# Attention over heads in a four-layer transformer: projections copied into another ring, later marks for statistics and gates, and the last two tiles of tokens woven together

## The chip, the cores and the metric

The kernel runs on one core of a Trainium2 chip. The metric is the time of one execution on the device in microseconds (us). Three runs of the kernel before gave 2483.38, 2484.43 and 2485.16 us; their median is 2484.43 us. The profile comes from a further execution.

## The reference

The input x has 4 batches of 512 tokens with 288 channels; four layers follow one another. Every layer makes six vectors from a condition, normalises, attends, multiplies by a gate and adds, then does the same with an MLP of 1152 hidden channels (layer 0 has four experts, of which each token takes two). Layers 0, 1 and 3 attend over tokens. Layer 2 attends over heads: for each token the 16 heads of 18 channels attend to one another, and the result is transposed and reshaped across tokens. Cut to what matters:

```python
def layer_2(x, c):
    ada = silu(c) @ ada_w + ada_b
    shift_msa, scale_msa, gate_msa, shift_mlp, scale_mlp, gate_mlp = split(ada, 6)
    x = x + gate_msa * attention(modulate(layernorm(x), shift_msa, scale_msa))
    x = x + gate_mlp * mlp(modulate(layernorm(x), shift_mlp, scale_mlp))
    return x

def attention(x):
    qkv = (x @ qkv_w + qkv_b).reshape(n, t, 3, 16, 18)
    q, k, v = qkv[:, :, 0], qkv[:, :, 1], qkv[:, :, 2]
    attn = softmax(einsum('nthd,ntkd->nthk', q * 18 ** -0.5, k))
    out = einsum('nthk,ntkd->nthd', attn, v)
    out = out.transpose(0, 2, 1, 3).reshape(n, t, d)
    return out @ proj_w + proj_b
```

## The kernel before, in words

All values are float32, and x stays on chip. A batch is four tiles of 128 tokens, so there are 16 tiles. Instructions are issued in an order which the program itself sets: loops over the large work (attention of a layer, half MLPs of two tiles) call `gap()` (L139) at every block, and `gap` and `follow` (L152) put pieces of other work into these places. That other work consists of generators: a list of tasks with due times, and for layer 2 the lists `chain` and `beside`. A generator yields the cost that it has used up; `follow` adds a credit at each gap (RATE, 1.1 us, L52) and takes pieces while credit is left. `mark(key, delay)` (L99) says that a value is ready so many gaps later, and `until` (L920) holds a generator back until then. So a mark shifts where in each engine's program an instruction stands; every engine runs its own program in order.

Attention over heads is `attention_over_heads` (L809). It runs beside the MLP of layer 1 (batches 1 to 3) and that of layer 2, both written by `half_mlp` (L1638): nine hidden blocks, for each an `up` (L1650, and L1657 for the last channels; ACT's gelu L1661) and a `down` (L1669, L1672), and at the end the copy upd_m by ACT (L1683), its gating (L1684) and its addition to x (L1685) on GpSimd.

For each tile i, with heads in four groups g:

- `kept` (L822, matmuls L829): three groups of matmuls on TensorE give queries, keys and values; keys and values are copied by ACT (L838), queries are read where they are.
- `weigh`: VectorE multiplies queries and keys (pq, L847) and reduces the products to scores (hs, L853). The scores have a ring of three buffers (L845, tag "hs").
- `shift`: VectorE finds the maximum (L857) and subtracts it (L858). After every second tile ACT takes the exponentials of both (L1001).
- `weighted`: GpSimd multiplies weights and values (pv, L863; ring "ex" of four buffers). `summed`: VectorE reduces them (ho, L875). `denominators`: VectorE (L879, L880). `finish`: GpSimd divides (ho, L887) and SP writes the tile to a scratch area in DRAM (L888).

`stream` (L961) orders this: in its round i it weighs tile i, multiplies values for tile i − 2 and sums tile i − 3. After the last tile of a batch, `after(b)` (L940) reads the rows back from the scratch area (`read`, L892), transposes them (`turned`, L905), projects them (`project`, L912) with a copy upd_a by ACT (L916), gates (L917) and adds to x (L918), and then starts the norm for the layer's MLP. `before(b)` does the norm ahead of the attention. `norm` (L429) takes statistics on VectorE (L435, L436), their scalars on GpSimd (L443 to L446) and the scaling on ACT (L458); `chunks` (L486) transposes its result on TensorE (L501).

The copies upd_a and upd_m share the ring "upd" of two buffers. Layer 3's attention, which begins while layer 2 ends, writes queries and keys through a ring "qc" of three buffers, from which SP spreads them by transfers (L598). Its weights are loaded by `load_attention` (L228, transfers L247 to L256), and its first scores and maxima are L608 and L623. `gating` (L399, matmuls L406, copies L407) makes the gates and `modulation` (L367; L351, L357, L359, L389, L391) the six vectors.

The rounds of the stream that the diff replaces end with

```python
                if i >= 3:
                    finish(i - 3)
                    if (i - 3) % TB == TB - 1:
                        beside.append([after((i - 3) // TB), False])
```

Of the kernel before, what the change touches and what calls it, by code (L numbers as in the profile page):

```python
# [10 lines left out]
F32 = mybir.dt.float32  # L11
# [8 lines left out]
P = 128  # L20
# [38 lines left out]
def tile_dit_blocks(ctx: ExitStack, tc: tile.TileContext, x_in, cond_t, sel_den, sel_b, w_gate, layers, out):  # L59
# [39 lines left out]
    def mark(key, delay=1):  # L99
        ready[key] = flow["now"] + delay  # L100
# [708 lines left out]
    def attention_over_heads(l):  # L809
# [50 lines left out]
        def weighted(i, g):  # L860
            hs = slice(g * GH, (g + 1) * GH)
            prod = work.tile([P, GH, HD, NH], F32, tag="ex", bufs=4, name=f"pv_{l}_{i}_{g}")
            nc.gpsimd.tensor_tensor(  # L863
                prod,
                sc[i][:, hs, :].unsqueeze(2).to_broadcast([P, GH, HD, NH]),
                qkv[i][:, 1].rearrange("p h d -> p d h").unsqueeze(1).to_broadcast([P, GH, HD, NH]),
                ALU.mult,
            )
            pv[i, g] = prod

        def summed(i, g):
            hs = slice(g * GH, (g + 1) * GH)
            if g == 0:
                o[i] = work.tile([P, NH, HD], F32, tag="ho", bufs=2, name=f"ho_{l}_{i}")
            nc.vector.tensor_reduce(o[i][:, hs, :], pv.pop((i, g)), AX.X, ALU.add)  # L875

        def denominators(i):
            den = o["den", i] = small.tile([P, NH, 1], F32, tag="hd1", name=f"hd1_{l}_{i}")
            nc.vector.tensor_reduce(den, sc[i], AX.X, ALU.add)  # L879
            nc.vector.reciprocal(den, den)  # L880
# [27 lines left out]
        def project(b, t):  # L908
            pp = other()[:, :C]
            for k in range(NK):  # L910
                n = KP + (1 if k == NK - 1 else 0)
                nc.tensor.matmul(  # L912
                    pp, rt[b][:n, k, t * P : (t + 1) * P], w["wp"][:n, k, :], start=k == 0, stop=k == NK - 1
                )
            upd = work.tile([P, 2, C], F32, tag="upd", bufs=2, name=f"upd_a_{l}_{b}_{t}")
            nc.scalar.copy(upd[:, 0, :], pp)  # L916
            nc.gpsimd.tensor_tensor(upd[:, 0, :], upd[:, 0, :], gates[l, 0][:, b, :], ALU.mult)  # L917
            nc.gpsimd.tensor_tensor(x[:, b * TB + t, :], x[:, b * TB + t, :], upd[:, 0, :], ALU.add)  # L918

        def until(*keys):  # L920
            while any(ready.get(key, 1 << 30) > flow["now"] for key in keys):
# [18 lines left out]
        def after(b):  # L940

            for _ in range(3):
                yield WAIT
            read(b)
            for _ in range(3):
                yield WAIT
            yield from until(("gate", l, 0), ("projection", l))
            for k in range(NK):
                yield BANK
                turned(b, k)  # L950
                yield -0.9
            for t in range(TB):
                yield BANK
                project(b, t)
                yield -1.5
            mark(("x", l, 1, b), 6)
            yield from until(("x", l, 1, b))
            yield from norm(l, 1, b)
            yield from turn_normed(1, b)

        def stream():  # L961
            n = len(tiles)
            yield from until(("loaded", l), ("ht", l, 0, 0))
            for s in (1, 2, 0):
                if s:
                    yield BANK
                kept(0, s)
                yield -1.5
            beside.append([before(1), False])
            yield from until(("values free", l - 1, B - 1, TB - 1))  # L970
            del ready["cleared"]
            for i in range(n + 3):
                for g in range(4):
                    if i < n:
                        weigh(i, g)
                        yield 2.8
                        if g > 0 and i + 1 < n:
                            yield from until(("ht", l, 0, (i + 1) // TB))
                            if g < 3:
                                yield BANK  # L980
                            kept(i + 1, g % 3)
                            yield -1.5
                    if g == 1 and 2 <= i < n + 2:
                        denominators(i - 2)
                        yield 0.7
                    if i >= 3:
                        summed(i - 3, g)
                    if 2 <= i < n + 2:
                        weighted(i - 2, g)
                    yield 1.4 if i >= 3 else 0.0  # L990
                if i >= 3:
                    finish(i - 3)
                    if (i - 3) % TB == TB - 1:
                        beside.append([after((i - 3) // TB), False])
                if i < n:
                    shift(i)
                    if i % TB == TB - 2:
                        mark(("first products", l, i // TB), 1)
                    if i % 2:
                        for j in (i - 1, i):  # L1000
                            nc.scalar.activation(sc[j], sc[j], AF.Exp)  # L1001
                    yield 1.0
                if i % TB == 0 and 2 <= i // TB + 1 < B:
                    beside.append([before(i // TB + 1), False])
            mark(("over heads", l))
            mark(("all spread", l))
            yield from clear()
# [630 lines left out]
    def half_mlp(l, b, half, hook=None):  # L1638

        h, w, gate = ht[l, 1, b], w_mlp[l, 0], gates[l, 1]  # L1640
        func = AF.Gelu if l == 2 else AF.Gelu_apprx_tanh
        PY, UP = 0, 2
        US = 0.3
        s = slice(half * BT, (half + 1) * BT)

        def up(fs):
            for j, f in enumerate(fs):
                full = w["w1"][f // 3][0]
                for k in range(KF):
                    nc.tensor.matmul(  # L1650
                        banks[:, UP + j, :BT], full[:, k, (f % 3) * P : (f % 3 + 1) * P], h[:, k, s],
                        start=k == 0, stop=False,
                    )
                gap(US)
            for j, f in enumerate(fs):
                r = slice((f % 3) * RC, (f % 3 + 1) * RC)
                nc.tensor.matmul(banks[:, UP + j, :BT], w["w1"][f // 3][1][r, :], h[r, KF, s], start=False, stop=True)  # L1657
            hid = []
            for j, f in enumerate(fs):
                t = work.tile([P, S], F32, tag="ot", bufs=7, name=f"hid_{l}_{b}_{half}_{f}")[:, :BT]  # L1660
                nc.scalar.activation(t, banks[:, UP + j, :BT], func, bias=w["b1"][:, f : f + 1])  # L1661
                hid.append(t)
            return hid

        def down(fs, hid):
            if fs[0] == 0:
                for t in range(2):
                    r = slice(t * HP, t * HP + 1)
                    nc.tensor.matmul(banks[:, PY + t, :C], ones[r, :], w["b2"][r, :], start=True, stop=False)  # L1669
            for f, hf in zip(fs, hid):  # L1670
                for t in range(2):
                    nc.tensor.matmul(  # L1672
                        banks[:, PY + t, :C], hf[:, t * P : (t + 1) * P], w["w2"][f // 3][:, f % 3, :],
                        start=False, stop=f == NF - 1,
                    )
                if f < NF - 1:
                    gap(US)
                if hook is not None and f % 3 == 2:
                    hook(f // 3)
            if fs[-1] == NF - 1:  # L1680
                t0 = b * TB + 2 * half
                y = work.tile([P, 2, C], F32, tag="upd", bufs=2, name=f"upd_m_{l}_{b}_{half}")
                nc.scalar.copy(y, banks[:, PY : PY + 2, :C])  # L1683
                nc.gpsimd.tensor_tensor(y, y, gate[:, b : b + 1, :].to_broadcast([P, 2, C]), ALU.mult)  # L1684
                nc.gpsimd.tensor_tensor(x[:, t0 : t0 + 2, :], x[:, t0 : t0 + 2, :], y, ALU.add)  # L1685
                if half == 1:
                    mark(("x", l + 1, 0, b), 5)
                gap(US)

        for fs in DUOS:  # L1690
            hid = up(fs)
            if pending_down:
                pending_down.pop()()
            pending_down.append(lambda fs=fs, hid=hid: down(fs, hid))
# [28 lines left out]
    for l in range(n_layers):  # L1723
# [15 lines left out]
        if l == 1:  # L1739
            before.append(("token mod", B - 1))  # L1740
        task(products, base + 40, [("ada", l, 1, 3)] + before, modulation(l, 1))
        before = [("x", l, 0, B - 1)] if l else []
        task(products, base + 60, [("gate row", l, 1)] + before, gating(l, 1))
        if l == OVER_HEADS:
            due = starts["attention", l - 1] + 2 * (LEAD + N_STEPS - 14)
# [181 lines left out]
```

## Time and profile before

| | |
|---|---|
| median of three runs | 2484.43 us (2483.38 to 2485.16) |
| the profiled execution | 2486.91 us, of which its span is 2485.2 us |
| TensorE busy (PE) | 2291.2 us, 92% of the span |
| weights loaded to TensorE (PEld) | 1218.6 us, 49% |
| VectorE busy (DVE) | 1086.3 us, 44% |
| ScalarE busy (ACT) | 834.8 us, 34% |
| GpSimd busy (POOL) | 521.4 us, 21% |
| first multiplication of tile 0, of tile 15 of layer 2's attention | at 1369.83 us, at 1714.36 us |
| last finish of a tile (L887) | ends at 1780.35 us |
| first scores of layer 3 (L608) | at 1945.54 us |

Times are microseconds from the start of the span. A line of a timeline has the start, the duration, the engine, the line in the code, the operation, what it writes and reads with the shapes, and in brackets how long the engine was idle before it and who released it. SPq is SP's queue of transfers. A line of waits has the engine and line that waited, for whom, the sum in us, how often and the longest. The page's second part cuts the span in 40 slices; a digit is a slice's busy share in tenths.

### The profile page before, as it was taken

The numbers are of one execution on the slowest core, as the hardware profiler recorded it, in microseconds if no ns is written. First come the engines' busy times: TensorE is split into PE (matmuls) and PEld (weight loads), VectorE is DVE, ScalarE is ACT, GpSimd is POOL, SyncE is SP. The second block draws the span as 40 slices with busy tenths as digits, with TensorE's granted clock in tenths as the row PEclk, the third lists the DMA queues.
The fourth block names the chain that finished last, engine by engine and source line by source line (L and its number), as shares of the span: only waits on it lengthen the run. The fifth ranks groups of instructions, "written<-read, shape, count | busy, mean of one in ns | idle before, by whom it ended". The sixth has DMA issues, their size and how long they took to land. (4 is left out here: it accounts for less than half of the span.)

```text
span 2485.2 us, 30140 instructions
## 1 busy us (share of the span) xinstructions
PE 2291.2 (92%) x11188; PEld 1218.6 (49%) x11188; DVE 1086.3 (44%) x1955; ACT 834.8 (34%) x1233; POOL 521.4 (21%) x517
## 2 busy tenths in 40 slices
PE   5899999899998999999999999778589999999998
PEld 2333333367776773333353677455456433333455
DVE  2445655441012025555524669989210455555100
ACT  1244434422221223344426233323223244444311
POOL 2000020321022111100010257778621100011000
PEclk9699999999999997899999899888799799999999
DMA  5201110446554541000000001100110000000000
GB/s 143 97 30 62 38 36 12 107 161 189 177 160 152 175 124 62 13 14 16 28 21 1 22 3 32 36 17 17 22 56 2 28 16 16 14 14 6 1 20 20
DMA packets 163033, 134.23 MB, mean 54 GB/s; under 512 B 81365, under 2 KB 146725, under 8 KB 162886
## 3 DMA queue, kind: packets, MB, share of 16 engines
q1 hardware_dynamic: 159814, 122.86, 17.0%
q0 software_dynamic: 3072, 9.44, 1.2%
q8 instruction: 89, 1.46, 0.2%
q14 instruction: 58, 0.48, 0.1%
HBM read 90.67 MB, written 26.25 MB: 47 GB/s over the span
## 5 line engine op out<-in xcount | busy, mean ns | idle before, releaser
L660 DVE TENSOR_REDUCE mx<-banks 128x1 f32<-128x512 f32 x696 | 447.8, 685 | 370.9 <-PE banks L608 370.3
L608 PE MATMUL banks<-qk 32*128 32x512 f32 x3072 | 548.8, 681 | 11.8 <-DVE mx L660 7.0
L653 ACT ACTIVATE ex<-banks 128x1024 f32<-128x1024 f32 x348 | 356.4, 1024 | 513.2 <-PE banks L608 511.9
L608 PEld LDWEIGHTS banks<-qk 32*128 32x128 f32 x3072 | 180.5, 194 | 230.6 <-DVE mx L660 97.7
L863 POOL TENSOR_TENSOR pv<-hs,qk 128x1152 f32<-128x1152 f32 x64 | 203.7, 3196 | 50.2 <-DVE ho L875 35.3
L682 PE MATMUL banks<-ex,va 128*32 128x512 f32 x1536 | 212.2, 623 | 0.0
L1462 PE MATMUL banks<-w_b,hid_b 128*128 128x288 f32 x684 | 187.6, 417 | 0.0
L555 PE MATMUL banks<-ht,wqk 96*128 96x512 f32 (+1 forms) x360 | 186.7, 629 | 0.6 <-DVE upd_a L515 0.6
L1650 PE MATMUL banks<-ht,w 128*128 128x256 f32 x504 | 134.3, 402 | 38.2 <-ACT hid L1661 37.6
L1442 PE MATMUL banks<-block,w_b 128*128 128x256 f32 x684 | 165.8, 387 | 3.6 <-DMA w_b<-in_w 2.9
L702 POOL COPY rec<-r 128x512 f32<-128x512 f32 x48 | 29.6, 616 | 659.9 <-DVE r L698 586.2
L1672 PE MATMUL banks<-w,hid 128*128 128x288 f32 x504 | 151.8, 437 | 0.0
L1454 ACT ACTIVATE hid_b<-banks,b_b 128x256 f32<-128x256 f32 x171 | 68.7, 473 | 241.1 <-PE banks L1448 163.1
L1462 PEld LDWEIGHTS banks<-w_b,hid_b 128*128 128x128 f32 x684 | 123.9, 191 | 49.9 <-issue 21.9
L1442 PEld LDWEIGHTS banks<-block,w_b 128*128 128x128 f32 x684 | 129.3, 193 | 31.2 <-issue 11.4
L1650 PEld LDWEIGHTS banks<-ht,w 128*128 128x128 f32 x504 | 98.8, 201 | 61.7 <-ACT hid L1661 41.9
L719 PE MATMUL banks<-wp,ot 128*128 128x288 f32 x384 | 118.9, 435 | 5.9 <-DVE upd_a L515 3.5
L1672 PEld LDWEIGHTS banks<-w,hid 128*128 128x128 f32 x504 | 93.4, 198 | 46.3 <-issue 26.3
L516 POOL TENSOR_TENSOR x<-x,upd_a 128x288 f32<-128x288 f32 x48 | 38.1, 793 | 364.6 <-DVE upd_a L515 337.1
L555 PEld LDWEIGHTS banks<-ht,wqk 96*128 96x128 f32 (+1 forms) x360 | 61.4, 189 | 100.1 <-issue 86.2
L719 PEld LDWEIGHTS banks<-wp,ot 128*128 128x128 f32 x384 | 68.6, 195 | 76.1 <-issue 51.9
L682 PEld LDWEIGHTS banks<-ex,va 128*32 128x32 f32 x1536 | 31.1, 109 | 152.4 <-issue 150.6
(224 smaller groups left out, 2574.9 us busy)
## 6 DMA issues: line engine op xcount, KB each, us to landing
w_b<-in_w SPq DMA_DIRECT2D x57, 432.0 KB
w_b<-in_w SPq DMA_DIRECT2D x57, 384.0 KB
qk<-qc SPq DMA_DIRECT2D x336, 38.0 KB
wa<-in_wada SPq DMA_DIRECT2D x7, 864.0 KB
block<-x_mem SPq DMA_DIRECT2D x19, 288.0 KB
y_mem<-y_b SPq DMA_DIRECT2D x19, 288.0 KB
x_mem<-zeros SPq DMA_DIRECT2D x7, 768.0 KB
y_mem<-zeros SPq DMA_DIRECT2D x7, 768.0 KB
```

The source lines that it names most:

```text
L555: nc.tensor.matmul(to, st(rows, k), mv(rows, k), start=k == 0, stop=k == NK - 1)
L608: nc.tensor.matmul(to, qk[u][r, of, c * P : (c + 1) * P], qk[u][r, 1 - of, :], start=True, stop=True)
L653: nc.scalar.activation(e, WEIGHTS, AF.Exp)
L660: nc.vector.tensor_reduce(mxs[mu % 2][:, mc, h : h + 1], pm[j], AX.X, ALU.max)
L682: nc.tensor.matmul(SUMS[j * HP : (j + 1) * HP, :], vas[0][:, c, at : at + HP], ex[step, j // 2][:, j % 2, :], start=c == 0, stop=c == TB - 1,)
L719: nc.tensor.matmul(pp, done[b * NG + g][:, t * P : (t + 1) * P], w["wp"][:, g, :], start=g == 0, stop=g == NG - 1)
L863: nc.gpsimd.tensor_tensor(prod, sc[i][:, hs, :].unsqueeze(2).to_broadcast([P, GH, HD, NH]), qkv[i][:, 1].rearrange("p h d -> p d h").unsqu ...
L1442: nc.tensor.matmul(banks[:, UP + j, :BT], w1[:, k, j * P : (j + 1) * P], hx[i][:, k, :], start=k == 0, stop=False)
L1454: nc.scalar.activation(t, banks[:, UP + j, :BT], AF.Gelu_apprx_tanh, bias=b1[:, f : f + 1])
L1462: nc.tensor.matmul(banks[:, PY + t, :C], hid[j][:, t * P : (t + 1) * P], w2[:, j, :], start=f == 0, stop=f == NF - 1)
L1650: nc.tensor.matmul(banks[:, UP + j, :BT], full[:, k, (f % 3) * P : (f % 3 + 1) * P], h[:, k, s], start=k == 0, stop=False,)
L1672: nc.tensor.matmul(banks[:, PY + t, :C], hf[:, t * P : (t + 1) * P], w["w2"][f // 3][:, f % 3, :], start=False, stop=f == NF - 1,)
```

## The change

There are three parts. The projection's copy upd_a moves from the ring "upd" to the ring "qc". Marks come later: a batch's x after attention over heads from 6 to 9 gaps, x after the second half of a batch's MLP from 5 to 12 gaps, and a new mark "gated" 25 gaps after it, on which the second gates of layer 2 wait in place of x. The stream has one round less; in the ordinary rounds a group of sums comes ahead of the products with the values (`usual`), and the sums, products and finishes of the last tiles follow a table (`last`).

```diff
@@ project
-            upd = work.tile([P, 2, C], F32, tag="upd", bufs=2, name=f"upd_a_{l}_{b}_{t}")
-            nc.scalar.copy(upd[:, 0, :], pp)
-            nc.gpsimd.tensor_tensor(upd[:, 0, :], upd[:, 0, :], gates[l, 0][:, b, :], ALU.mult)
-            nc.gpsimd.tensor_tensor(x[:, b * TB + t, :], x[:, b * TB + t, :], upd[:, 0, :], ALU.add)
+            upd = work.tile([P, S], F32, tag="qc", bufs=3, name=f"upd_a_{l}_{b}_{t}")[:, :C]
+            nc.scalar.copy(upd, pp)
+            nc.gpsimd.tensor_tensor(upd, upd, gates[l, 0][:, b, :], ALU.mult)
+            nc.gpsimd.tensor_tensor(x[:, b * TB + t, :], x[:, b * TB + t, :], upd, ALU.add)
@@ after
-            mark(("x", l, 1, b), 6)
+            mark(("x", l, 1, b), 9)
@@ stream
-            for i in range(n + 3):
+            usual = {g: [f"s1{g}", f"w0{g}"] + (["d0"] if g == 1 else ["f1"] if g == 3 else []) for g in range(4)}
+            last = {
+                0: ["s30", "s31", "w00", "w01", "d0"], 1: ["s32", "s33", "f3", "w02", "w03", "s00", "w10"],
+                2: ["s01", "w11", "s02", "w12"], 3: ["d1", "s03", "w13", "f0"], 4: ["s10", "s11", "s12", "s13", "f1"],
+            }
+            for i in range(n + 2):
                 for g in range(4):
                     if i < n:
                         weigh(i, g)
...
-                    if g == 1 and 2 <= i < n + 2:
-                        denominators(i - 2)
-                        yield 0.7
-                    if i >= 3:
-                        summed(i - 3, g)
-                    if 2 <= i < n + 2:
-                        weighted(i - 2, g)
-                    yield 1.4 if i >= 3 else 0.0
-                if i >= 3:
-                    finish(i - 3)
-                    if (i - 3) % TB == TB - 1:
-                        beside.append([after((i - 3) // TB), False])
+                    for what in usual[g] if i < n else last.get((i - n) * 4 + g, ()):
+                        if i < n:
+                            j = i - 2 - int(what[1])
+                        else:
+                            j = n - 3 if what[1] == "3" or what == "f3" else n - 2 + int(what[1])
+                        if j < 0:
+                            continue
+                        if what[0] == "w":
+                            weighted(j, int(what[2]))
+                        elif what[0] == "s":
+                            summed(j, int(what[2]))
+                            yield 1.4
+                        elif what[0] == "d":
+                            denominators(j)
+                            yield 0.7
+                        else:
+                            finish(j)
+                            if j % TB == TB - 1:
+                                beside.append([after(j // TB), False])
@@ half_mlp
                 if half == 1:
-                    mark(("x", l + 1, 0, b), 5)
+                    mark(("x", l + 1, 0, b), 12)
+                    mark(("gated", l, b), 25)
@@ the tasks of each layer
-        before = [("x", l, 0, B - 1)] if l else []
+        before = [("gated", 1, B - 1) if l == OVER_HEADS else ("x", l, 0, B - 1)] if l else []
         task(products, base + 60, [("gate row", l, 1)] + before, gating(l, 1))
```

## The prediction, on record before the result

> **What bounds the kernel now.** I read the page first (parts 1 and 2), then a table of busy time by stretches, then the sums of waits, then the timelines of single engines around the longest waits.
>
> ```profile
> span 2485.2 us, 30140 instructions
> PE   5899999899998999999999999778589999999998
> DVE  2445655441012025555524669989210455555100
> POOL 2000020321022111100010257778621100011000
> ```
>
> A slice is 62 us. TensorE is at 9 tenths nearly everywhere, except in slices 26 to 30 (about 1550 to 1865 us). There VectorE and GpSimd stand at 7 to 9 tenths: this is the attention over heads of layer 2, beside the MLPs of layers 1 and 2. The stretches (columns: us, then busy time of PE, PEld, DVE, ACT, POOL with counts, clock, DMA share, GB/s) show where each limit rules:
>
> ```profile
> 1440.00:1460.00 20.00, 20.00 (x91) 14.40 (x91) 1.88 (x7) 4.47 (x10) 3.39 (x5) 1.00 0.00 1
> 1500.00:1580.00 80.00, 75.47 (x336) 52.75 (x336) 74.59 (x79) 26.93 (x51) 61.47 (x33) 0.97 0.26 49
> 1580.00:1620.00 40.00, 24.88 (x77) 17.34 (x77) 37.55 (x45) 12.86 (x24) 31.74 (x27) 0.76 0.07 8
> 1740.00:1780.00 40.00, 27.28 (x108) 19.51 (x107) 16.18 (x21) 10.59 (x20) 36.08 (x26) 0.84 0.07 8
> 1780.00:1800.00 20.00, 9.43 (x35) 6.29 (x34) 0.00 (x0) 3.17 (x5) 5.24 (x8) 0.67 0.43 50
> 1810.00:1945.00 135.00, 133.92 (x548) 90.89 (x544) 8.98 (x28) 40.49 (x82) 23.11 (x31) 0.96 0.11 34
> ```
>
> Up to 1580 TensorE is full but VectorE's chain of 16 tiles already sets the later end; from 1580 to 1740 VectorE is the limit (37.6 of 40), from 1740 to 1780 GpSimd (36.1 of 40), then SP's transfers, and from 1810 to 1945 TensorE again (133.9 of 135). So a microsecond on the stream of tiles before 1780 moves the end; TensorE work moved from before 1808 to after it does too.
>
> What VectorE waited for between 1360 and 1960 (us in total, times, longest):
>
> ```profile
> DVE st L435 <- POOL x L1685: 67.6, 4, 24.2
> DVE pq L847 <- PE banks L829: 18.8, 7, 5.0
> DVE hd L879 <- POOL ho L887: 10.6, 1, 10.6
> DVE hs L853 <- POOL pv L863: 8.8, 5, 2.4
> ```
>
> Of the 67.6 us only the first lies inside the stream (it ends at 1458.0, 18.5 us long); the others end at 1838.5, 1884.7 and 1907.1, when VectorE has nothing urgent. The places that matter (start, us, engine, line, and in brackets the idle time before with its releaser):
>
> ```profile
> 1458.02 0.46 DVE L435 BATCH_NORM_STATS2 st<-x 128x6 f32<-128x288 f32 x1 [18.52 <-POOL x L1685]
> 1476.73 1.36 DVE L847 TENSOR_TENSOR pq<-banks,qk 128x1152 f32<-128x1152 f32 x1 [4.31 <-PE banks L829]
> ...
> 1482.77 1.40 POOL L1684 TENSOR_TENSOR upd_m<-upd_m,gate 128x576 f32<-128x576 f32 x1 [9.81 <-ACT upd_m L1683]
> 1779.67 0.68 POOL L887 TENSOR_TENSOR ho<-ho,hd 128x288 f32<-128x288 f32 x1
> ...
> 1804.10 0.40 SPq L892 DMA_DIRECT2D rows<-scratch  x1
> 1808.29 1.06 PE L905 MATMUL banks<-ident,rows 128*96 128x128 f32 x4 [18.86 <-DMA rows<-scratch]
> ```
>
> The last line is the chain's hinge: the last tile's finish (L887) ends at 1780.35, SP then issues the weights of layer 3 (L247 to L256) until 1804.1, only then the read of the rows, and TensorE stands still 18.9 us for it.
>
> **What the Trainium skill says.** "Perfetto Trace Analysis", Optimization Strategy: a kernel can have regimes with different limiting engines, and gaps are to be sought on the limiting one within its regime; the table above agrees. "SBUF — State Buffer", SBUF: two separate sides: GpSimd and VectorE share one port pair as an exclusive lock, which a VectorE operation with two SBUF inputs needs. The trace agrees: the subtraction L858 takes 0.43 us alone and up to 3.2 us (3.18 at 1469.2) where pv (L863, 3.2 us) runs beside it. "TensorE: Matmul & The Clock Gate", What's actually happening: after idling the array runs at half clock for some microseconds; here the clock is 0.67 and lower between 1780 and 1810.
>
> **The change part by part.** I compared the instruction order of both kernels, engine by engine. Up to about 1436 us they are the same.
>
> *Later marks.* VectorE's order around the statistics of layer 2, batch 1, is unchanged: the 18.5 us stall at 1458 stays. What moves is on TensorE: the transposes of that batch go from after hidden block 3 to after block 7 of the running half MLP. In between lie: up 1.8, w1r 0.6, four blocks of down 4.1, up 1.0, w1r 0.6 (start to start in TensorE's timeline) = 8.1 us. The queries and keys of tile 4 (L829) follow: their third group ended at 1476.5, and now about 1485.4 (from block 8, due at 1476.8, with three groups of 1.5, up 1.9, w1r and bias 1.3, one block 1.1). Also, on GpSimd the update of x by the MLP (upd_m, 1.4 + 1.4 us) now stands ahead of pv of tile 1 (three of 3.2) and waits, as before, for ACT's copy, which comes about 1477.6. So pv of tile 1 ends at 1477.7 + 2.9 + 3 × 3.2 = 1490.2. VectorE's first reduction of tile 4 needs that buffer of scores (L845, three of them): 1490.3 against 1478.2, **+12.1 us**. (By TensorE alone it would be 8.9.) Queued behind it on VectorE is the whole stream.
>
> Of this, the later waits for L829 at tiles 5, 6 and 7 (1.5, 2.4 and 0.2 us in VectorE's timeline) vanish, since TensorE is then ahead: 12.1 − 4.2 = 7.9. The modulation's VectorE work moves from tile 8 to tile 10 (−2.65, then +2.1 and a wait of about 0.95): +0.4. The statistics of layer 3, batch 0, leave the tiles before the last exponentials (2.3 + 0.4 us): −2.7. The stream stands at **+5.6** when the last exponentials (before: 1738.4) run.
>
> *Gates later, first tiles.* A mark only shifts where instructions are issued; it adds no wait on the chip. VectorE's and TensorE's work is the same and in the sum above; on SP only the read of batch 0's rows moves, ahead of one write of tile 4, and nobody waits for that write. Their cover is TensorE's idle time (15 of 40 us at 1580 to 1620); without it some 5 us.
>
> *The burst.* GpSimd's work from the exponentials on is: 8 × 3.14 pv, 4 × 1.6 upd_a (L917, L918), two ho 1.3, statistics' scalars 1.9, the last ho 0.7 = 35.4, with small gaps 35.8. Before it took 41.9 (1738.4 to 1780.35), because the MLP's update, another norm and the wait for ACT stood ahead of the last ho: **−6.1**. GpSimd is full in both, so pulling VectorE's reductions forward saves nothing by itself. SP keeps its order, the weights ahead of the rows, so rows are read 23.8 us after the finish as before. Rows arrive at −0.5.
>
> *TensorE behind the rows.* Since TensorE's program puts the rows' transposes earlier in the layer-2 MLP (after block 0 of batch 1's second half, not after block 3), three blocks (3.2), two ups (3.6), w1r (0.6) and nine transposes (1.3) that ran in the shadow of the stall now come after it: **+8.7**. From there TensorE is full until 1945, so it counts whole. If that cover were gone already, nothing would be lost.
>
> *Copies in the ring of qc.* Where upd_a waited for its buffer before (L916, L1683: 3.7 and 3.4 us, at 1751 and 1760), TensorE had slack: no gain on the path. In the new ring the copies of batch 3 meet layer 3's q and k, whose tiles are free only when SP has sent them: 36 transfers in 38.2 us (L598). The third copy would come some 45 us after the rows, the fifth tile's transfers end near 50. ACT waits 5 us there and behind it is gelu, which TensorE needs; it has about two blocks in hand. Bounds 0 and 6, taken **+3**.
>
> *Layer 3's start.* 2.3 us of statistics and the gate copies go behind 24 maxima (L623), where VectorE is late: **−2** (bounds 0 and −3).
>
> Sum: 5.6 − 6.1 + 8.7 + 3 − 2 = **+9.2**. The profiled execution took 2486.91 us (span 2485.2 and 1.7 around it), 2.5 above the median of 2484.43. So 2496.1 in its own terms, and 2493.6, say 2493.5, beside the median. Differences under 0.2% (5 us) a measurement hardly tells from no change.
>
> **The rivals.**
> 1. *The stream makes its delay good and more* (faster). After tile 4 it still had waits: 9.5 for L829 (1.5, 2.4, 0.2, and 4.1 and 1.2 at tiles 13 and 15) and 8.8 for pv. If all go: 12.1 − 18.3 + 0.4 − 2.7 = −8.5, and with a free ring −8.5 − 6.1 + 8.7 − 2 = −7.9: 2476.5. It decides if the last exponentials come more than 5.6 us earlier than before. For it: TensorE gets ahead by some us in the layer-1 MLP. Against: pv waits come from GpSimd's own pace, which is the same.
> 2. *The delay is just made good* (no change): stream 0, ring 0: −6.1 + 8.7 − 2 = +0.6: 2485.0. It holds if upd_m and tile 4 meet as late as before.
> 3. *The delay stays whole*: 12.1 + 0.4 − 2.7 at the exponentials, ring 6: 9.8 − 6.1 + 8.7 + 6 − 2 = +16.4: near 2501, with a slow clock after longer idling some 3 more, 2504. For it: the statistics' stall was not removed, which is also the sense in which the change doesn't do what it says.
>
> **How the numbers follow.** Forecast (+5 to +14): 0.46. Rival 1: 0.22. Rival 2: 0.20. Rival 3: 0.12. Range: from below rival 1 (2474) to rival 3 (2505). Faster 0.22, same 0.20, slower 0.58. The likeliest case alone: 2489.5 to 2498.5.
>
> **What would show it.** Right: the first L853 of tile 4 near 1490 with a wait on pv; the last exponentials near 1744; the last L887 under 36.5 us after them; TensorE idle before L905 longer than 18.9 us (about 27) and its arrival within 2 us of 1808; layer 3's first L608 some 9 to 10 us after 1945.5. Wrong: exponentials at or before 1738, or TensorE waiting in other places between 1810 and 1950, or the time between rows and L608 not longer.

## The result and the profile after

The changed kernel takes 2495.93 us (median of six runs) against 2484.8 us of the kernel before (six runs, the three known ones among them). The ratio is 1.0059 with a 95% interval of 1.004 to 1.0078: slower by about 0.6%. The forecast was 2493.5 us, slower by 0.36%.

The page of the changed kernel (profiled execution: 2494.08 us), the same lines as before. Behind the change its line numbers are 14 higher: L1664, L1671, L1675, L1686, L1697 to L1699 and L1015 are what L1650, L1657, L1661, L1672, L1683 to L1685 and L1001 were.

```profile
span 2492.4 us, 30130 instructions
PE   5899999899999999999998999578399999999998
DVE  2445666440021124655433748888210455555100
POOL 2000021230012110110010347778611100011000
```

TensorE's trough is one slice narrower and deeper (5, 7, 8, 3): the stall has moved together at the end of the stream. The span is only 7.2 us longer, but this understates the change. Both programs issue the same work up to this stage, and yet in the profile of the changed kernel layer 2's attention begins 10.2 us earlier: its first L847 is recorded at 1359.4 us against 1369.6. From there to layer 3's first scores (L608) the kernel before takes 576.0 us, the changed one 593.1: **+17.1**. From L608 to the end it is 539.7 and 539.9. All experiments below are read in this stretch too, since the early part differs from execution to execution.

The stretches of the changed kernel (us, busy time of PE, PEld, DVE, ACT, POOL with counts, clock, DMA share, GB/s):

```profile
1460.00:1480.00 20.00, 20.00 (x97) 15.09 (x96) 1.73 (x2) 9.17 (x16) 12.61 (x6) 1.00 0.00 1
1740.00:1780.00 40.00, 15.93 (x58) 10.72 (x57) 16.14 (x27) 4.95 (x11) 36.95 (x30) 0.70 0.25 15
1780.00:1800.00 20.00, 6.24 (x35) 4.46 (x34) 0.00 (x0) 6.23 (x12) 7.80 (x11) 0.74 0.40 61
1810.00:1945.00 135.00, 131.86 (x552) 90.42 (x550) 8.87 (x28) 41.00 (x82) 23.06 (x31) 0.95 0.09 28
```

VectorE now idles from 1460 to 1480 too (1.7 of 20), after the statistics' stall. The waits of VectorE, 1360 to 1960:

```profile
DVE pq L847 <- PE banks L829: 29.1, 4, 15.6
...
DVE hs L853 <- POOL pv L863: 21.6, 9, 5.0
```

The wait for tile 4's matmuls grew to 15.6 us, and the waits for pv from 8.8 to 21.6 us. The places, in VectorE's, GpSimd's, SP's and TensorE's timelines (add 10.2 us to compare with before):

```profile
1447.84 0.46 DVE L435 BATCH_NORM_STATS2 st<-x 128x6 f32<-128x288 f32 x1 [18.51 <-POOL x L1699]
1475.05 1.36 DVE L847 TENSOR_TENSOR pq<-banks,qk 128x1152 f32<-128x1152 f32 x1 [15.57 <-PE banks L829]
1479.63 1.35 DVE L853 TENSOR_REDUCE hs<-pq 128x64 f32<-128x1152 f32 x1 [3.22 <-POOL pv L863]
...
1467.31 1.40 POOL L1698 TENSOR_TENSOR upd_m<-upd_m,gate 128x576 f32<-128x576 f32 x1 [16.14 <-ACT upd_m L1697]
1470.16 9.44 POOL L863 TENSOR_TENSOR pv<-hs,qk 128x1152 f32<-128x1152 f32 x3
...
1737.32 6.32 POOL L863 TENSOR_TENSOR pv<-hs,qk 128x1152 f32<-128x1152 f32 x2
1772.05 0.67 POOL L887 TENSOR_TENSOR ho<-ho,hd 128x288 f32<-128x288 f32 x1
...
1797.49 0.40 SPq L892 DMA_DIRECT2D rows<-scratch  x1
1801.66 1.06 PE L905 MATMUL banks<-ident,rows 128*96 128x128 f32 x4 [14.90 <-DMA rows<-scratch]
1851.97 3.25 PE L912 MATMUL banks<-wp,rt 96*128 96x288 f32 x6 [3.08 <-ACT upd_a L916]
```

The statistics still wait 18.5 us. Tile 4 begins 8.5 us later (1475.05 + 10.2 against 1476.73), and its first reduction waits 3.2 us more for pv of tile 1, which upd_m holds up: 1479.63 + 10.2 = 1489.8. In the kernel before it was:

```profile
1478.19 1.35 DVE L853 TENSOR_REDUCE hs<-pq 128x64 f32<-128x1152 f32 x1
```

And a wait is there that was not on the path before: the projection's matmuls for ACT's copy upd_a.

### The profile page after: what moved, and what is told of

The parts are those of the page before. It is cut to its first block, busy times and chain, and to the rows that moved or that the text cites. A ratio compares the mean times of both kernels' runs of the same rounds, so it can differ in the third digit from the quotient of the medians.

```text
span 2492.4 us, 30130 instructions
## 1 busy us (share of the span) xinstructions
PE 2275.3 (91%) x11188; PEld 1212.6 (49%) x11188; DVE 1073.3 (43%) x1955; ACT 831.3 (33%) x1231; POOL 520.9 (21%) x517
## 3 DMA queue, kind: packets, MB, share of 16 engines
q1 hardware_dynamic: 159814, 122.86, 17.1%
## 5 line engine op out<-in xcount | busy, mean ns | idle before, releaser
L608 PE MATMUL banks<-qk 32*128 32x512 f32 x3072 | 541.4, 674 | 12.0 <-DVE mx L660 7.4
L608 PEld LDWEIGHTS banks<-qk 32*128 32x128 f32 x3072 | 178.8, 192 | 228.0 <-DVE mx L660 98.4
L1664 PE MATMUL banks<-ht,w 128*128 128x256 f32 x504 | 132.9, 398 | 46.2 <-ACT hid L1675 45.8
L1686 PE MATMUL banks<-w,hid 128*128 128x288 f32 x504 | 149.2, 433 | 0.0
L1664 PEld LDWEIGHTS banks<-ht,w 128*128 128x128 f32 x504 | 98.4, 200 | 69.4 <-ACT hid L1675 48.6
L1686 PEld LDWEIGHTS banks<-w,hid 128*128 128x128 f32 x504 | 92.5, 195 | 46.9 <-issue 27.2
L829 PE MATMUL banks<-wqk,ht 96*128 96x288 f32 (+1 forms) x288 | 84.9, 438 | 21.6 <-ACT upd_a L916 20.4
```

The source lines that it names most:

```text
L608: nc.tensor.matmul(to, qk[u][r, of, c * P : (c + 1) * P], qk[u][r, 1 - of, :], start=True, stop=True)
L829: nc.tensor.matmul(to, h[:n, k, t * P : (t + 1) * P], w["wqkv"][:n, k, s * C : (s + 1) * C], start=k == 0, stop=k == NK - 1,)
L1664: nc.tensor.matmul(banks[:, UP + j, :BT], full[:, k, (f % 3) * P : (f % 3 + 1) * P], h[:, k, s], start=k == 0, stop=False,)
L1686: nc.tensor.matmul(banks[:, PY + t, :C], hf[:, t * P : (t + 1) * P], w["w2"][f // 3][:, f % 3, :], start=False, stop=f == NF - 1,)
```

## The experiments

Twelve kernels. For each the table gives the ratio of times to the kernel before, and from the profile, counted from the first record of L847: the end of the last exponentials, the end of the last L887 ("finish"), the first L905 of batch 3 after it ("rows") and the first L608 of layer 3 ("scores").

| kernel | ratio, 95% interval | exponentials | finish | rows | scores |
|---|---|---|---|---|---|
| before | 1 | 369.1 | 410.8 | 438.7 | 576.0 |
| changed | 1.0059 (1.004 to 1.0078) | 374.8 | 413.3 | 442.3 | 593.1 |
| e1 ring alone | 1.0018 (1.0005 to 1.0031) | 369.2 | 410.8 | 439.5 | 579.9 |
| e2 changed, old ring | 1.0042 (1.0025 to 1.0058) | 376.3 | 414.8 | 445.0 | 588.6 |
| e3 stream loop alone | 0.999 (0.9976 to 1.0003) | 372.6 | 412.9 | 468.1 | 576.5 |
| e4 three marks alone | 1.0042 (1.0027 to 1.0056) | 380.0 | 418.6 | 477.1 | 585.7 |
| e5 mark 12 alone | 1.0073 (1.0052 to 1.0094) | 378.7 | 431.6 | 460.2 | 599.8 |
| e6 changed, without mark 12 | 1.006 (1.0039 to 1.0081) | 371.1 | 408.5 | 439.6 | 589.4 |
| e7 before, weights early | 0.9917 (0.9892 to 0.9941) | 369.1 | 410.7 | 442.7 | 556.1 |
| e8 e7 with the stream loop | 0.9926 (0.9905 to 0.9947) | 369.1 | 407.1 | 444.8 | 559.7 |
| e9 changed, without mark 12, old ring | 1.0028 (1.001 to 1.0046) | 371.2 | 408.6 | 438.8 | 582.4 |
| e10 changed, weights early | 1.0035 (1.0014 to 1.0056) | 392.1 | 427.3 | 441.2 | 583.9 |
| e11 mark 9 alone | 0.9993 (0.9978 to 1.0009) | 369.9 | 407.9 | 435.8 | 578.3 |
| e12 gated alone | 1.0013 (1.0 to 1.0026) | 371.1 | 412.7 | 440.7 | 577.3 |

Each ratio is against runs of the kernel before made alongside (medians 2484.0 to 2492.6 us). Its interval is 3 to 6 us wide to either side; the other columns are from one profile of each kernel, and how far they repeat was not measured. Counted to the end of the span, their differences from the kernel before agree with those of the times within 6 us. So what is said below of smaller differences rests on the lines of single profiles.

The whole stretch to the end of the span, of which the expectations speak, is the last column plus 539.5 to 541.8 us. (The first two expectations count from the start of the first L847, 0.3 us after its first record.)

### e1, e2: the ring

e1 puts this into the kernel before; e2 takes it out of the changed one:

```diff
-            upd = work.tile([P, 2, C], F32, tag="upd", bufs=2, name=f"upd_a_{l}_{b}_{t}")
+            upd = work.tile([P, S], F32, tag="qc", bufs=3, name=f"upd_a_{l}_{b}_{t}")[:, :C]
...
```

> The kernel before with one part alone: the projection's copies in the ring of qc. Measured from the first multiplication of tile 0 of layer 2's attention (L847) to the end of the span, which leaves out the first 1370 us (before 1115.4 us, changed 1132.8). My theory (late transposes and TensorE's order behind the rows are the main costs, the ring a small one): 1118, with ACT's fourth or third copy of batch 3 waiting some us. Rival (the ring is the main cost of the 13.6 us that the changed kernel needs more between the rows and layer 3's first scores): 1123 or more.

> The changed kernel with the copies back in the ring upd; all else changed. Same stretch. My theory: 1130, 3 us under the changed kernel. Rival (the ring is the main cost): 1122 to 1124.

Measured: e1 1121.6 for the stretch, nearer to the rival's 1123 than to my 1118: the scores come 3.9 us later, near my size of 3, and another 2.0 us are lost behind them (541.7 against 539.7), which need not be the ring's, since e7 has them too without it. e2: 1128.9, so 4.5 for the scores when the ring is taken out; in the changed kernel it is more than a small cost and less than the rival's 9 to 11. The mechanism is seen on ACT, changed kernel:

```profile
1843.55 0.40 ACT L916 COPY upd_a<-banks 128x288 f32<-128x288 f32 x1 [2.81 <-DMA qk<-qc]
...
1851.52 0.70 ACT L916 COPY upd_a<-banks 128x288 f32<-128x288 f32 x2 [6.30 <-DMA qk<-qc]
1856.29 0.40 ACT L916 COPY upd_a<-banks 128x288 f32<-128x288 f32 x1 [4.08 <-DMA qk<-qc]
```

The copies wait 2.8, 6.3 and 4.1 us for the transfers of layer 3's queries and keys, which SP sends one after another. TensorE stands only 3.1 us for it, but its clock falls. The 15 us that begin some 45 us behind the rows, changed kernel first, then e2 (the last figures are clock, DMA share and GB/s):

```profile
1847.00:1862.00 15.00, 11.92 (x35) 7.76 (x34) 2.98 (x10) 1.84 (x5) 7.87 (x12) 0.66 0.41 120
```

```profile
1859.00:1874.00 15.00, 15.00 (x70) 10.90 (x69) 2.98 (x10) 3.12 (x9) 8.15 (x12) 1.00 0.44 121
```

35 matmuls at clock 0.66 against 70 at 1.00. From rows to scores the changed kernel takes 150.8 us and e2 143.6, both with 596 matmuls: the ring costs 7.2 there. The pair without the mark of 12, e6 and e9, says nearly the same (149.8 and 143.6, with a stall of 3.1 us in e6). In the order of the kernel before the ring costs 3.1 there (140.4 in e1 against 137.3): TensorE waits 1.0 us for a copy and 2.9 us for a gelu, and its clock stays full after that (1.00 from 1864 to 1876). Some of it comes back earlier, since in e2 exponentials and rows come 1.5 and 2.7 us later.

### e3, e4: the stream loop and the marks

e3 is the new loop of `stream` alone, e4 the three marks alone.

> The kernel before with the new loop of the stream alone (sums ahead of products, burst at the end). The instruction order puts the rows' transposes behind layer 3's first matmuls and four hidden blocks later than before, while SP's order stays: the weights of layer 3 still go out after the last finish. My theory (what decides is when weights and rows land and how much TensorE work stands behind them): the finish comes 5.5 us earlier, first L555 near 1799 instead of 1812.5, 5 us more work behind it: 1107. Rival (the burst itself is what costs, because sums and products meet on the shared port): 1120 or more.

> The kernel before with the three marks alone (9, 12, gated 25), old stream loop and old ring. My theory: tile 4 starts 8 to 12 us later, the last exponentials about 9 later, weights in place about 3 later, 10 us more TensorE work behind them, rows' transposes late in the program: 1120. Rival (marks alone are free, the loss comes from the burst or the ring): 1113 to 1116.

e3: 1116.0, no measurable difference; I had expected 1107 and was wrong. The order on TensorE is as said (rows come 29 us later in it, after layer 3's first products), but the exponentials end 3.5 us later and the finish 2.1 us later, not 5.5 earlier. TensorE then waits for a norm (ACT's xh) and for the weights in place of the rows:

```profile
1796.13 2.03 PE L501 MATMUL banks<-ident,xh 128*128 128x128 f32 x4 [11.54 <-ACT xh L458]
1812.23 4.80 PE L555 MATMUL banks<-ht,wqk 96*128 96x512 f32 x6 [12.15 <-POOL wqk L277]
...
1843.65 0.60 PE L905 MATMUL banks<-ident,rows 128*96 128x128 f32 x4
```

The rival (1120 or more) fails too: no cost of the burst is measured. e4: 1125.6, more than either theory said, with the exponentials 10.9 us late where I had 9.

### e5, e6: the mark of 12 gaps

```diff
-                    mark(("x", l + 1, 0, b), 5)
+                    mark(("x", l + 1, 0, b), 12)
```

> The kernel before with one mark alone: x after a batch's MLP ready 12 gaps later instead of 5. From the first multiplication of tile 0 of layer 2's attention to the end of the span (before 1115.7, changed 1133.0, three marks together 1125.6). My theory (this mark delays the transposes that tile 4 waits for): tile 4 at 115.6 to 116 us after tile 0 instead of 107, the last exponentials 8 to 11 later, TensorE's order behind the rows unchanged: 1124 to 1126. Rival (the other marks do it): 1116 to 1118.

> The changed kernel with this one mark back at 5 gaps. Same stretch. My theory: no delay at tile 4; the last exponentials 5 to 6 us before those of the changed kernel, rows' transposes as early in TensorE's program as there: about 1126. Rival (the other parts make up for the delay, what counts is TensorE's order behind the rows): 1131 to 1133.

e5: 1139.4. The mark alone costs 23.8 us at the scores, more than the whole change, and more than my theory's 9. The exponentials are 9.6 later, as in the theory; the rest is GpSimd's order. The last ho stands behind the MLP's update, and this waits for a TensorE that is late (it has waited 23.2 us for ACT's gelu, L1661, in front of which ACT's norm, L458, waits for GpSimd):

```profile
1780.12 0.67 POOL L887 TENSOR_TENSOR ho<-ho,hd 128x288 f32<-128x288 f32 x1
1789.05 1.40 POOL L1684 TENSOR_TENSOR upd_m<-upd_m,gate 128x576 f32<-128x576 f32 x1 [8.26 <-ACT upd_m L1683]
...
1796.96 0.40 POOL L477 COPY xh<-xh 128x256 f32<-128x256 f32 x1 [3.00 <-ACT xh L458]
1797.33 0.67 POOL L887 TENSOR_TENSOR ho<-ho,hd 128x288 f32<-128x288 f32 x1
```

From the exponentials to the finish it takes 52.9 us, against 41.7 before and 38.5 in the changed kernel, where the last ho stands ahead of the update. e6: 1129.2, between my 1126 and the rival's 1131. In the changed kernel this mark is worth only 593.1 − 589.4 = 3.7 us, and the times (1.006 and 1.0059) don't tell the two apart. Tile 4 is on time again in e6, as expected, but another wait takes the delay's place: at tile 10 VectorE stands 6.6 us for TensorE's part of the six vectors (L357 for L351; 0.6 us in the changed kernel), and tile 14 starts 7.5 us late all the same (14.3 in the changed kernel).

### e7, e8: the weights of layer 3 ahead of the last tiles

The kernel before, with none of the change; e8 adds the stream loop.

```diff
-        mark(("loaded", l), 6)
+        mark(("loaded", l), 24 if l == 3 else 6)
...
                             kept(i + 1, g % 3)
                             yield -1.5
+                            if i + 2 == n and g == 3:
+                                mark(("all spread", l), 8)
...
             mark(("over heads", l))
-            mark(("all spread", l))
```

> The kernel before with layer 3's attention weights sent out as soon as the last tile's queries and keys are computed, so ahead of the last four tiles' writes on SP, and their scaling on GpSimd kept behind the last finish. Nothing of the change is in it. My theory (weights and rows behind the last finish are the hinge): TensorE no longer stands still before the rows, layer 3's first scores come up to 18 us earlier, 1098 to 1101. Rival (TensorE is short of other work there, the stall moves to the next wait): 1108 to 1116.

> The same with the new loop of the stream. My theory: the finish no longer decides, so the burst adds little: 1097 to 1101, within 2 us of the run without it. Rival (the burst is worth its 3 to 5 us once the weights are out of the way): 3 us or more below the run without it.

e7: 1097.8, at the low end of my 1098 to 1101, and 2466.86 us over all against 2488.41 alongside, 0.83% less: **the fastest version found**. SP sends the weights while GpSimd still multiplies, and only the last write stands ahead of the rows' read, which follows 6.4 us after it. TensorE has layer 3's products to do and reaches the rows without a wait for them:

```profile
1739.58 0.63 SPq L251 DMA_DIRECT2D wqk<-in_bqk  x1
1740.32 37.28 SPq L888 DMA_DIRECT2D scratch<-ho  x4
1784.02 0.36 SPq L892 DMA_DIRECT2D rows<-scratch  x1
```

```profile
1784.82 2.74 PE L555 MATMUL banks<-ht,wqk 96*128 96x512 f32 x6
...
1809.12 0.64 PE L905 MATMUL banks<-ident,rows 128*96 128x128 f32 x4 [0.28 <-ACT qc L580]
```

e8: 1101.3. The stream loop gains 3.6 us at the finish (407.1), and nothing comes of it: the scores are 3.6 us later than in e7, as the finish no longer decides and TensorE waits elsewhere (10.8 us for xh, L501, at 1790). That is more than the 2 us that I allowed, on the other side from the rival's, which fails.

### e9, e10: what is left of the change

e9 has the loop, mark 9 and gated; e10 is the changed kernel with the edit of e7.

> The changed kernel without the copies' new ring and without the mark of 12 gaps: new stream loop, mark 9, gated 25. TensorE's program has the same order from the rows on as in the changed kernel. From tile 0's first multiplication of layer 2's attention: first scores of layer 3 at 576.0 us before, 593.1 changed, 588.6 without the ring, 589.4 without the mark of 12. My theory (order behind the rows costs 6 of its own, ring 4 to 7, mark 12 the rest): last finish at 408 to 409, first scores at 580 to 583. Rival (ring and mark are all there is to it): 575 to 577.

> The changed kernel with layer 3's attention weights sent early as in the run before that had it (first scores there at 556.1 after tile 0). My theory: the last finish is hidden once TensorE has other work before the rows, so the delay of the stream and the order behind the rows cost little and what is left is the ring's 4 to 7 us: 557 to 564. Rival (the loss of the change is in the stream and stays): 570 or more.

e9: finish 408.6 and scores 582.4, both as expected. From rows to scores it takes 143.6 us where the kernel before takes 137.3, without a wait of TensorE between them in the trace: 596 matmuls in place of 552. So TensorE's order behind the rows costs 6.3 us. e10 (583.9) is far from my 557 to 564. It lies in the rival's range (570 or more), but the traces show another cause than the rival's: here the weights stand ahead of the read of batch 2's rows on SP (1716 to 1739), TensorE waits 19.4 us for those and the exponentials come 12 us after GpSimd ran out of work. The stall was moved one batch up, so this run doesn't tell what the change costs once the weights are out of the way; that stays open.

### e11, e12: the other marks alone

> The kernel before with only the mark after attention at 9 gaps instead of 6. In the instruction order the last norm of batch 2 goes behind the last finish on GpSimd, the MLP's update stays ahead; 1.3 us more TensorE work stand behind the rows. My theory: finish 3 to 6 us earlier after the exponentials, first scores of layer 3 at 571 to 575 after tile 0 (before 576.0). Rival (this mark delays the norms and so the MLP of layer 2): 578 or more.

> The kernel before with only the second gates of layer 2 awaiting the new mark of 25 gaps. The six vectors' VectorE work moves from tile 8 to a later tile; nothing else moves near the end. My theory: first scores of layer 3 within 1.5 us of 576.0 after tile 0. Rival (the gates' later place disturbs the stream): 578 or more.

e11: the finish comes 2.9 us earlier, as expected, but the scores 2.3 later, against my 571 to 575: from rows to scores it takes 142.5 us, with 12 more transposes (L501) and 2.1 us of waiting for ACT's copies of qc. Over all it is not to be told from no change. e12: scores +1.3, as expected.

## Why the prediction was right, and where it was not, term by term

| step of the sum | predicted | measured | from |
|---|---|---|---|
| stream at the last exponentials | +5.6 | +5.7 | changed against before |
| exponentials to finish | −6.1 | −3.2 | 38.5 against 41.7 |
| finish to rows | 0 | +1.1 | 29.0 against 27.9 |
| order behind the rows | +8.7 | +6.3 | e9 |
| ring, behind the rows | +3 | +7.2 | 150.8 against 143.6 (e2) |
| layer 3's start | −2 | +0.2 | 539.9 against 539.7 |
| sum | +9.2 | +17.3 | |

The sign was right, and each delay that the sum named is in the trace. The time landed inside the likeliest case's own range. But the medians differ by 11.1 us, the ratio says 0.59%, and the stretch says 17.3 us (0.70%, still inside the interval): nearly twice the sum. Two terms were mis-sized above all, the burst by 2.9 us and the ring by 4.2, and layer 3's start by 2.2. That the median came within 2.4 us of the forecast is therefore in part luck: it has the early part in it, which varies by more than that.

- **Later marks.** Right for tile 4: predicted first reduction 12.1 us later and at 1490.3, measured 11.6 and 1489.8, with both causes (TensorE, then pv behind upd_m). Less right on the way: I had the stream at about 8 us late from tile 7 on; tiles 10 to 14 are 12 to 15 late. New waits for L829 and pv of 5.0 us each at tiles 7 and 8 were missed. The last tiles won back more than the 2.7 us that I gave them. That the sum at the exponentials fits to 0.1 us is partly luck, since its course on the way was another; and as e6 shows, only 3.7 of the 5.7 us go away with the mark of 12.
- **The burst.** "36.5 us after the exponentials" was wrong: 38.5. GpSimd needed 35.4 us from the first pv of tile 14, as worked out, but it was still 3.1 us behind with tile 13 when the exponentials were done (pv at 1730.2 to 1736.7). I had let it start at once. And the burst alone (e3) gains nothing. What shortened the way to the finish is that the wait for a norm (3.0 us, L477) and, in the changed kernel, the update too no longer stand ahead of the last ho. The new loop isn't needed for that: with the marks alone (e4) it takes 38.5 us too, with the mark of 9 alone (e11) 38.1.
- **TensorE behind the rows.** Right in kind, 2.4 us too large: 44 more matmuls, 6.3 us. Some of the difference is the clock, whose mean over this stretch was 0.97 in e9 and 0.96 before.
- **Copies in the ring of qc.** Right in kind, with the wait on ACT for SP's transfers, but 7.2 against 3, beyond my upper bound of 6. ACT waited three times, not once, 13.2 us in all, and the price of TensorE's 3.1 us stall is doubled by the half clock that follows it. The size of 3 would have been right in the old order (e1).
- **Layer 3's start.** No gain (+0.2 in place of −2); the runs don't show why.
- **Rivals.** Rivals 1 and 2 are out: no run with the mark of 12 shows the delay made good at the exponentials. Rival 3 had the size (+16.4 against 17.3) and the ring's 6 us, but not the path: it kept the whole delay to the exponentials (9.8), and there the measured one is 5.7. What I called the hinge, SP's weights ahead of the rows, is confirmed by e7: 19.9 us at the scores.
- **The signs named.** Two came: tile 4's first reduction with its wait for pv, and the exponentials at 1744.4 (1734.2 + 10.2). The others didn't: the last L887 came 38.5 us after the exponentials, not under 36.5; the rows reached TensorE at 1811.8, 3.5 us late and not within 2; the scores came 17 us late, not 9 to 10; and TensorE stood 14.9 us before L905, not 27. A sign of being wrong came too, TensorE's new wait between 1810 and 1950, for the copy upd_a. The idle time that was expected before the rows is there, only earlier: TensorE waits for a gelu that ACT issues behind a norm, and this stands behind tile 15's products on GpSimd. From the exponentials to the rows its waits come to some 41 us, 32 before. The earlier wait costs nothing by itself, as TensorE still waits for the rows after it.

```profile
1774.67 3.78 PE L1664 MATMUL banks<-ht,w 128*128 128x256 f32 x8 [24.07 <-ACT hid L1675]
```

- **Readings.** Three were loose, without weight in the sum. VectorE and GpSimd stand at 7 to 9 tenths in slices 26 to 28 alone (2 and 6, then 1 and 2 tenths in the last two). L858 takes up to 3.33 us beside pv, not 3.2. The end of tile 4's matmuls, worked out from the steps given, is 1485.6 and not 1485.4; by TensorE alone tile 4 came 8.5 us later.

Why the marks cost here: the stream's generator itself waits until the transposes of the next batch are issued. The mark of 5 gaps put them at the moment when their input was ready (L501 at 1463.61, ACT's xh done at 1463.54, before). Seven gaps more only hold up TensorE's matmuls of tile 4, and with them VectorE. The runs show this without exception: tile 4 starts 115.7 us after the first record of L847 in the five kernels with the mark of 12 (changed, e2, e4, e5, e10) and 107.2 us after it in all others.

The single parts don't add up: 3.9 (ring) + 0.5 (loop) + 9.7 (marks) = 14.1 against 17.1, and one mark alone costs more than all three (23.8 against 9.7), since GpSimd's order at the finish depends on which of them are there: in e5 the MLP's update stands between the last two ho, in e4 it doesn't.

## What to carry to other kernels

When a mark or a due time shifts where work is issued, look at each engine's order for what comes to stand ahead of the last link of the chain (here the last ho on GpSimd, the rows' read on SP), and price that, not the shift. Before giving a copy another ring, ask who frees that ring's tiles and at what rate; a ring fed by a queue of transfers makes a fast engine wait at the queue's pace. When loads stand between the last result and its reader on one queue, sending them earlier can be worth more than all work on the stream (e7: 0.83%), provided that nothing due sooner is queued behind them (e10).

## What the runs showed of the hardware

- The first 1360 us, which none of the edits touches, took 1355.9 us (e10) to 1381.0 us (e4) until the first record of L847, a spread of 25 us. From there to the statistics' stall it is 88.4 or 88.5 us in each of them. Effects of a few microseconds are better read from a stretch of the profile than from the whole time.
- A stall of TensorE of 3.1 us was followed by a stretch with a mean clock of 0.66, in which 15 us held half the matmuls (35 against 70). The Trainium skill, "TensorE: Matmul & The Clock Gate", What's actually happening, says that an idle window brings the half clock and that busy time takes it away again; these lines agree. So a short wait of TensorE can cost twice its length (7.2 us here, 6.3 for one of 3.1 in e6). It doesn't always: after a wait of 2.9 us in e1 the clock stayed at 1.00.
- The half clock also came without a wait. In e9 TensorE was busy from 1850 to 1859 throughout, at clock 1.00, and then had 0.50 from 1859.7 to 1863. Just before stand the eight small matmuls of the gates (L406, 4x288, 1856.5 to 1858.9). So it is in the kernel before: the gates' matmuls from 1862.4 to 1865.1, then 0.50 from 1865 to 1871, with no wait of TensorE above 0.7 us in the 50 us before. Whether they bring it was not tested.
